# Four graph layers in one kernel: the fourth layer's transposes taken from TensorE to VectorE squares and DMAs, and the second layer's Newton step to GpSimd

## The chip, the cores and the metric

The kernel runs on one core of a Trainium2 chip. The metric is the device time of one execution in microseconds (us); the median of three runs of the kernel before is 2920.45 us (2920.34 to 2920.62). A profile is one execution recorded instruction by instruction on the engines of the core: TensorE (PE for matmuls, PEld for loading its weights), VectorE (DVE), ScalarE (ACT), GpSimd (POOL) and SyncE (SP, which here only starts DMAs).

## The reference, cut to what matters

A graph of N = 4096 nodes with 256 features passes through four layers. Each adds its result to its input and normalises each row:

```python
x = _layernorm(x + _L0_gnn_ref(x, adj, W0, a0))               # four heads, additive scores
x = _layernorm(x + _L1_gnn_ref(x, adj, Wq, bq, Wk, bk, Wv, bv))  # four heads, dot products
x = _layernorm(x + _L2_gnn_ref(x, adj, W2, a2))               # one head, additive scores
x = _layernorm(x + _L3_gnn_ref(x, adj, Wq3, Wk3))             # cosine scores
```

The fourth layer is the one that the change is mostly about:

```python
Qn = _cos_normalize(features @ Wq.T)      # 4096 x 128, rows of length 1
Kn = _cos_normalize(features @ Wk.T)
raw_att = Kn @ Qn.T                       # 4096 x 4096
att = jax.nn.softmax(jnp.where(adj > 0, raw_att, NEG), axis=1)
prop_fea = att @ features
return 0.5 * prop_fea + 0.5 * features
```

The layernorm divides by the root of the variance. The kernel gets the inverse root as exp(-0.5 ln v) on ScalarE and improves it by one Newton step, r (1.5 - 0.5 v r r): the four small instructions of `end_root`.

## The kernel before, in words

The features stay in SBUF for the whole run, in X: 32 tiles of 128 rows (nodes), 256 columns and one column of twos. Every layer walks over 8 blocks b of 512 target nodes, and within a block over the source tiles. One step of the walk is a unit (b, j): get the weights of the source tile j for the targets of block b (ScalarE), mask them by the adjacency (VectorE), multiply them with the values and add into PSUM (TensorE). In layers one, three and four a block has 32 units of 128 sources; in layer two 64 units of 64 sources. The sums run one to three units behind the weights.

**Layer two** (`multi_head_attention`, lines 509 to 782). TensorE makes scores (L622) and sums (L655), ScalarE takes the exponential (L624), VectorE masks (L634). The sums of weights for the softmax are gathered in den: GpSimd adds every even unit (L641), an accumulating DMA started by GpSimd adds every odd one (L647). What is left to do for block b - 1 is strewn into the units of block b by `finish`: the variance is ready at unit 29 (`begin_root`, L151, and ScalarE's L130 and L131), `end_root` (L137 to L140) stands at unit 33 of the block, and the scaling of the four row tiles (L155) at 35, 37, 39 and 41. The order on PE, DVE and ACT is the order of the program there (`manual_schedule`); GpSimd's instructions are placed by the scheduler.

**Layer three** (`additive_one`, lines 382 to 506). ScalarE makes e (L432), VectorE masks it to prob (L434), TensorE adds 4 x (128x128)x(128x257) products per unit into PSUM (L440). There are three buffers of prob. PE's order is that of the program; the other engines' orders are the scheduler's. SP loads the masks (L430). In block b the outputs of block b - 1 are finished at units 0, 4, 8 and 12.

**Layer four** is prepared by the class `Cosine` for a block b in three steps (`prepare`, L810):
- step 0: `transposed_block` turns the 4 x 2 squares of 128x128 of the features by TensorE with the identity (L118) into two PSUM banks, which VectorE and ScalarE copy to xT (L120);
- step 1: TensorE multiplies xT with the weights of q and k (L823), ScalarE takes the squares of the rows' lengths (L828), VectorE copies the rows (L829), makes the inverse root (L831, L137 to L140) and scales (L834);
- step 2: TensorE turns q and k (L840), ScalarE copies them to T (L841), which holds q and k of all nodes, turned.

Six of the blocks are prepared in the last block of layer three: step 0 of block n at unit 4n, step 1 at 4n + 2, step 2 at 4n + 5 (L497), so that a turn of four units of sums holds one of each. Blocks 6 and 7 are prepared within the first block of layer four itself, at units 1, 3, 6 and 12, 14, 17 (L892). The masks of layer four are loaded by GpSimd's queue (L808), the first three behind layer three's units 6, 10 and 14 (`behind`, which makes GpSimd copy a number of the unit first, L91).

**The walk of layer four** (`cosine_attention`): scores T x T (L864, into banks p and g), exponential (L867), mask (L868), sums with X (L875). The outputs are stored by SP (L888), and y, their buffer, is filled by ScalarE (L905).

Of the kernel before, what the change touches and what calls it, by code (L numbers as in the profile page):

```python
# [9 lines left out]
FP = mybir.dt.float32  # L10
# [4 lines left out]
OP = mybir.AluOpType  # L15
# [3 lines left out]
P = 128  # L19
D = 256  # L20
KC = D // P
QB = 4
QW = QB * P
# [5 lines left out]
def kernel(  # L29
# [81 lines left out]

    def transposed_block(sb, bank, b, copies=(nc.vector.tensor_copy, nc.scalar.copy)):

        xT = sb.tile([P, KC, QW], FP, name="xT")
        pts = [bank() for _ in range(KC)]
        for c, pt in enumerate(pts):
            for k in range(QB):
                nc.tensor.transpose(pt[:, k * P:(k + 1) * P], X[:, b * QB + k, c * P:(c + 1) * P], ident)  # L118
        for c, pt in enumerate(pts):
            copies[c](xT[:, c, :], pt)  # L120
        return xT

    def one_row(mv, k, y):
        st = fin.tile([P, 6], FP, name="bn")
# [6 lines left out]
        nc.scalar.activation(r, r, AF.Exp, scale=-0.5)  # L131
        return r

    def end_root(v, r, n):

        s = fin.tile([P, n], FP, name=f"s{n}")
        nc.vector.tensor_tensor(s, r, r, OP.mult)  # L137
        nc.vector.tensor_tensor(s, s, v, OP.mult)
        nc.vector.tensor_scalar(s, s, -0.5, 1.5, OP.mult, OP.add)  # L139
        nc.vector.tensor_tensor(r, r, s, OP.mult)  # L140

    def inverse_root(v, n):

# [26 lines left out]
    def additive_values(xT, b, groups, w_sb, V, src, dst, H, slope):  # L170

        g = 1.0 - slope
        heads = "p k (h d) -> p k h d"
        for k, n, pw in groups:
            for c in range(KC):
                for i in range(n):
                    nc.tensor.matmul(pw[:, i, :D + 2 * H], xT[:, c, (k + i) * P:(k + i + 1) * P], w_sb[:, c, :],  # L177
                                     start=(c == 0), stop=(c == KC - 1))
            t = slice(b * QB + k, b * QB + k + n)
            s, d = pw[:, :, D:D + H], pw[:, :, D + H:D + 2 * H]  # L180
            nc.scalar.activation(src[:, t, :], s, AF.Exp, scale=g)
            nc.scalar.activation(dst[:, t, :], d, AF.Exp, scale=g)
            nc.scalar.activation(V[:, t, D:], d, AF.Exp, scale=slope)
            nc.vector.tensor_tensor(V[:, t, :D].rearrange(heads, h=H), pw[:, :, :D].rearrange(heads, h=H),
                                    V[:, t, D:].unsqueeze(3).to_broadcast([P, n, H, D // H]), OP.mult)
# [196 lines left out]
    def additive_one(w_sb, slope, tail, op, follow):  # L382
# [3 lines left out]
        with ExitStack() as lay:  # L386
# [76 lines left out]
            with tc.manual_schedule(engines={mybir.EngineType.PE}):  # L463
                xTs = {0: turn(0), 1: turn(1)}
                project(0, xTs[0])
                project(1, xTs[1], [0, 1])
                fill_row(0)
                project(1, xTs[1], [2, 3])
                for i in range(len(units) + 1):
                    if i < len(units):  # L470
                        b, j = units[i]
                        weights(b, j)

                        if b == 0 and j // QB + 2 < NB:
                            n = j // QB + 2
                            if j % QB == 0:
                                xTs[n] = turn(n)
                            elif j % QB == 2:
                                project(n, xTs[n])
                                fill_row(n)  # L480
                    if i:
                        b, j = units[i - 1]
                        sums(b, j)
                        if (b, j) == (0, 1):
                            fill_row(1)
                        if b == 0 and j in (0, 3, 5):
                            tail(bank, (0, 3, 5).index(j))
                            if j == 5:
                                follow.start()
                        if b and j % 4 == 0 and j // 4 < QB:  # L490
                            outputs(b - 1, j // 4)
                        if b == NB - 1:
                            if j in (6, 10, 14):
                                follow.load_mask(0, (j - 6) // 4, prob[b, j][:, :1])


                            for step, first in enumerate((0, 2, 5)):  # L497
                                if j >= first and (j - first) % 4 == 0 and (j - first) // 4 < NB - 2:
                                    follow.prepare(even_bank, (j - first) // 4, step)
                        if j == NT - 1:  # L500
                            take_all(b)
# [7 lines left out]
    def multi_head_attention(w_sb, b_sb, tail, rows_of_den, narrow_edges):  # L509
# [12 lines left out]
        with ExitStack() as lay:  # L522
# [7 lines left out]
            with ExitStack() as pro:  # L530
# [14 lines left out]
                def keys(b):  # L545
                    for n, to, scale in (("k", kT, 1.0), ("q", qT, qscale)):
                        for o in range(KC):
                            pk = bank()
                            for c in range(KC):
                                nc.tensor.matmul(pk, w_sb[n][:, c, o * P:(o + 1) * P], xTs[b][:, c, :],  # L550
                                                 start=(c == 0), stop=(c == KC - 1))
                            part = to[:, o, b * QW:(b + 1) * QW]
                            nc.scalar.activation(part, pk, AF.Identity, bias=b_sb[n][:, o:o + 1], scale=scale)
                            nc.vector.tensor_reduce(big[n][:, b, o:o + 1], part, AX.X, OP.max,
                                                    apply_absolute_value=True)

                def values(b):


                    for k in range(0, QB, KC):  # L560
                        pv = pv2.tile([P, KC, D], FP, name="pv")
                        for s in range(KC):
                            for c in range(KC):
                                nc.tensor.matmul(pv[:, s, :], xTs[b][:, c, (k + s) * P:(k + s + 1) * P], w_sb["v"][:, c, :],  # L564
                                                 start=(c == 0), stop=(c == KC - 1))
                        j = 2 * (b * QB + k)
                        for n in range(2):
# [149 lines left out]
            def finish(b, j):  # L717
# [12 lines left out]
                elif j == 18:  # L730
                    half(turned_half(halves(), b, 2), b, 2)
                elif j in (21, 23, 25, 27):
                    k = (j - 21) // 2
                    if k == 0:
                        mvs[b] = fin.tile([P, QB, 2], FP, name="mv")
                    one_row(mvs[b], k, rows[k])
                elif j == 29:
                    roots[b] = begin_root(mvs[b])
                elif j == 33:
                    end_root(*roots[b])  # L740
                elif j in (35, 37, 39, 41):
                    k = (j - 35) // 2
                    scale_row(rows[k], mvs[b], roots[b][1], k)
# [41 lines left out]
    class Cosine:  # L785
# [7 lines left out]
        def start(self):  # L793
# [1 line left out]
            self.pool = self.stack.enter_context(tc.tile_pool(name="co_in", bufs=2, side="right", reuse_waits="tile"))  # L795
            self.masks = self.stack.enter_context(tc.tile_pool(name="co_mask", bufs=4, side="right", reuse_waits="tile"))
            self.mask = {}
            self.T = keep.tile([P, 2, N], FP, name="T")
            self.w_sb = keep.tile([P, KC, 2 * P], FP, name="w3_sb")
            load_w(self.w_sb[:, :, :P], wq3T, nc.sync)  # L800
            load_w(self.w_sb[:, :, P:], wk3T, nc.sync)
# [7 lines left out]

        def prepare(self, bank, b, step):  # L810

            in_, w_sb, T = self.pool, self.w_sb, self.T
            if step == 0:
                self.xT[b] = transposed_block(in_, bank, b)
            elif step == 1:
                xT = self.xT.pop(b)
                norm = in_.tile([P, QB, 2], FP, name="norm")
# [1 line left out]
                for k in range(0, QB, 2):  # L819
                    pr = bank().rearrange("p (t n f) -> p t n f", t=2, f=P)  # L820
                    for t in range(2):
                        for c in range(KC):
                            nc.tensor.matmul(pr[:, t, :, :], xT[:, c, (k + t) * P:(k + t + 1) * P], w_sb[:, c, :],  # L823
                                             start=(c == 0), stop=(c == KC - 1))
                    for t in range(2):
                        for n in range(2):
# [7 lines left out]
                nc.vector.tensor_tensor(flat, flat, r.unsqueeze(2).to_broadcast([P, QB * 2, P]), OP.mult)  # L834
            else:
                rows = self.rows.pop(b)
                for n in range(2):
                    pt = bank()
                    for k in range(QB):
                        nc.tensor.transpose(pt[:, k * P:(k + 1) * P], rows[:, k, n, :], ident)  # L840
                    nc.scalar.copy(T[:, n, b * QW:(b + 1) * QW], pt)  # L841

    def cosine_attention(co, tail):
        MJ = co.MJ
        T, in_ = co.T, co.pool
        with ExitStack() as lay:
            sb = pool(lay, "co_sb", 3)

            pa = pool(lay, "co_pa", 1, space=PSUM)
            pz = pool(lay, "co_pz", 2, space=PSUM)  # L850
# [5 lines left out]
                return ps.tile([P, QW], FP, name="g")  # L856

            def weights(b, j):
                cols = slice(b * QW, (b + 1) * QW)
                m = b, j // MJ  # L860
                if m not in co.mask:
                    co.load_mask(*m)
                p = bank() if b and j % 2 else pz.tile([P, QW], FP, name="p")
                nc.tensor.matmul(p, T[:, 0, j * P:(j + 1) * P], T[:, 1, cols], start=True, stop=True)  # L864

                z = prob[b, j] = sb.tile([P, QW], FP, name="prob")
                nc.scalar.activation(z, p, AF.Exp)  # L867
# [21 lines left out]

            units = [(b, j) for b in range(NB) for j in range(NT)]  # L890
            LAG = 2
            steps = {(0, j + n): (NB - 2 + b, step) for b, j in enumerate((1, 12)) for step, n in enumerate((0, 2, 5))}  # L892
            for i in range(len(units) + LAG):
                if i < len(units):
                    b, j = units[i]
# [5 lines left out]
                if i >= LAG:  # L901
                    b, j = units[i - LAG]
                    if j == NT - 8:
                        y[b] = in_.tile([P, QB, D], FP, name="y")
                        nc.scalar.mul(y[b], X[:, b * QB:(b + 1) * QB, :D], 1.5)  # L905

                    if i < len(units):
# [93 lines left out]
```

## Time and profile before

| what | value |
|---|---|
| median of three runs | 2920.45 us |
| the profiled execution | 2920.01 us |
| its span, first to last instruction | 2918.1 us |
| granted TensorE clock | 0.999 |
| VectorE's masking in layer two, L634, 512 times | 1223 ns each |
| GpSimd's addition in layer two, L641, 248 times | 2495 ns each |
| TensorE per product of layers three and four with 257 columns (two records, from start to start) | 0.434 us |
| DVE, ACT, POOL busy in a turn of layer three's last block (2190 to 2202 us) | 6.3, 7.0, 0 of 12 us |
| POOL busy in a block of layer two (1103 to 1217 us) | 101 of 114 us |
| TensorE waiting for L634 in all | 5.6 us, 8 times |

A line of the profile names an engine, a source line, an operation, "out<-in" by the names of the tiles, a shape and how often it ran. The chain of work goes back from the last instruction, at each step to what released it, so an engine's share of the chain is what it holds of the time. The table of DMAs gives the size in KB and the median time from issue to landing, where it is known. A busy PE is a rough measure, since matmuls overlap and their ends are modelled: distances between starts are taken instead.

### The profile page before, as it was taken

How to read it: one execution, taken by the hardware profiler on the slowest of the kernel's cores; microseconds unless marked ns; L12 is line 12 of the kernel's file. 1: busy time of each engine (PE TensorE's matmuls, PEld its weight loads, DVE VectorE, ACT ScalarE, POOL GpSimd, SP SyncE). 2: the span in 40 equal slices, each digit the busy share in tenths (PEclk: the TensorE clock that was granted, in tenths of full speed). 3: DMA queues.
4: the chain of work that ended last, by engine and by line, in shares of the span. 5: the costliest groups of instructions: out<-in, count | busy, mean ns of one | idle time of the engine just before them, and what ended most of it. 6: DMA issues, size and time to landing. Idle time of an engine off the chain costs nothing.

```text
span 2918.1 us, 50377 instructions
## 1 busy us (share of the span) xinstructions
PE 2901.0 (99%) x20269; PEld 1564.5 (54%) x20269; DVE 1959.0 (67%) x2545; ACT 1668.3 (57%) x2613; POOL 927.0 (32%) x647
## 2 busy tenths in 40 slices
PE   9999999999999999999999999999999999999998
PEld 5333333333643333333333358888888777777776
DVE  8899999997677877877877765555655323333333
ACT  7899999997356666666666654444454222222222
POOL 0010010100068888988889860000000000000000
PEclk9999999999999999999999999999999999999999
DMA  7566666664068888889889874444442333333331
GB/s 204 107 135 140 136 140 142 135 134 84 1 142 191 182 187 189 181 186 191 180 189 188 184 164 138 153 152 150 154 136 60 49 58 58 58 58 58 58 58 29
DMA packets 207148, 374.94 MB, mean 128 GB/s; under 512 B 15057, under 2 KB 90817, under 8 KB 206018
## 3 DMA queue, kind: packets, MB, share of 16 engines
q0 software_dynamic: 102304, 177.77, 38.5%
q1 hardware_dynamic: 104336, 193.69, 20.2%
q8 instruction: 159, 2.61, 0.3%
q14 instruction: 75, 0.61, 0.1%
q10 hardware_dynamic: 274, 0.26, 0.0%
HBM read 317.07 MB, written 21.04 MB: 116 GB/s over the span
## 4 chain that ended last, share of the span: by engine, by line
PE 97%; DVE 2%; ACT 0%; issue 0%; DMA 0%; DVEq 0%; SPq 0%
PE acc L274 23%; PE acc L875 15%; PE p L622 15%; PE acc L655 14%; PE acc L440 8%; PE g L440 8%; PE p L864 4%; PE g L864 3%; PE g L550 2%; PE g L177 1%; PE pv L564 1%; PE g L118 1%; PE acc L823 1%; PE acc L177 1%; DVE prob L634 1%; DVE s L139 1%
## 5 line engine op out<-in xcount | busy, mean ns | idle before, releaser
L634 DVE TENSOR_TENSOR prob<-p,mask 128x1024 f32<-128x1024 f32 x512 | 623.0, 1223 | 197.2 <-ACT p L624 193.4
L624 ACT ACTIVATE p<-p,shift 128x1024 f32<-128x1024 f32 x512 | 556.2, 1088 | 331.9 <-PE p L622 331.0
L274 PE MATMUL acc<-prob,V 128*32 128x512 f32 x6144 | 664.0, 592 | 1.2 <-DVE prob L264 1.2
L641 POOL TENSOR_TENSOR den<-den,prob 128x1024 f32<-128x1024 f32 x248 | 618.8, 2495 | 72.4 <-DVE prob L634 62.9
L261 ACT ACTIVATE prob<-row,dst 128x512 f32<-128x512 f32 x1020 | 633.2, 712 | 0.1
L264 DVE SCALAR_TENSOR_TENSOR prob<-prob,mask 128x2048 f32<-128x2048 f32 x256 | 582.7, 2288 | 24.1 <-ACT prob L261 20.4
L622 PE MATMUL p<-qT,kT 64*64 64x512 f32 x4096 | 532.7, 590 | 5.6 <-DVE prob L634 5.6
L655 PE MATMUL acc<-prob,V 64*64 64x512 f32 x4096 | 531.5, 589 | 0.0
L875 PE MATMUL acc<-X,prob 128*128 128x257 f32 x2048 | 485.2, 380 | 0.0
L875 PEld LDWEIGHTS acc<-X,prob 128*128 128x128 f32 x2048 | 388.5, 190 | 160.7 <-issue 113.4
L868 DVE TENSOR_TENSOR prob<-prob,mask 128x512 f32<-128x512 f32 x256 | 176.5, 691 | 418.8 <-ACT prob L867 417.6
L274 PEld LDWEIGHTS acc<-prob,V 128*32 128x32 f32 x6144 | 197.3, 110 | 453.1 <-issue 434.2
L91 POOL COPY tick<-prob 128x1 f32<-128x1 f32 x35 | 39.8, 1136 | 1017.5 <-DVE prob L264 644.3
L432 ACT ACTIVATE e<-row,dst 128x512 f32<-128x512 f32 x256 | 184.2, 722 | 235.1 <-DVE prob L434 209.0
L655 PEld LDWEIGHTS acc<-prob,V 64*64 64x64 f32 x4096 | 155.9, 133 | 285.3 <-issue 278.1
L622 PEld LDWEIGHTS p<-qT,kT 64*64 64x64 f32 x4096 | 153.7, 133 | 284.4 <-issue 255.7
L434 DVE SCALAR_TENSOR_TENSOR prob<-e,mask 128x512 f32<-128x512 f32 x256 | 178.5, 698 | 185.7 <-PE acc L440 94.5
L808 POOL DMA_DIRECT2D mask<-in_adjT x64 | 47.5, 743 | 633.8 <-DVE prob L868 509.7
L647 POOL DMA_DIRECT2D den<-prob x240 | 225.9, 941 | 28.0 <-DVE prob L634 21.0
L867 ACT ACTIVATE prob<-p 128x512 f32<-128x512 f32 x144 | 85.8, 596 | 260.1 <-PE p L864 246.0
L440 PE MATMUL g<-V,prob 128*128 128x257 f32 x1024 | 225.6, 380 | 0.0
L440 PE MATMUL acc<-V,prob 128*128 128x257 f32 x1024 | 225.1, 380 | 0.0
(154 smaller groups left out, 1972.2 us busy)
## 6 DMA issues: line engine op xcount, KB each, us to landing
mask<-in_adjT SPq DMA_DIRECT2D x256, 512.0 KB
den<-prob POOLq DMA_DIRECT2D x240, 512.0 KB, 5.3
mask<-edges SPq DMA_DIRECT2D x256, 128.0 KB
mask<-in_adjT POOLq DMA_DIRECT2D x64, 512.0 KB, 5.6
edges<-in_adj POOLq DMA_DIRECT2D x32, 512.0 KB, 9.8
den<-prob SPq DMA_DIRECT2D x16, 512.0 KB
row<-far SPq DMA_DIRECT2D x7, 1024.0 KB
X<-in_x SPq DMA_DIRECT2D x7, 512.0 KB
```

The source lines that it names most:

```text
L261: nc.scalar.activation(z[:, h, :], r, AF.Relu, bias=-1.0, scale=dst[:, j, h:h + 1])
L264: nc.vector.scalar_tensor_tensor(z, z, 1.0, mask[m][:, j % MJ, :].unsqueeze(1).to_broadcast([P, H, QW]), OP.add, OP.mult)
L274: nc.tensor.matmul(acc[b][h * G:(h + 1) * G, n, :], part, prob[b, j][:, h, :], start=(j == 0), stop=(j == NT - 1))
L440: nc.tensor.matmul(acc[b][k][:, :D + 1], prob[b, j][:, k * P:(k + 1) * P], V[:, j, :], start=(j == 0), stop=(j == NT - 1))
L622: nc.tensor.matmul(p[c * d:(c + 1) * d, r, :], kT[half, c, j * d:(j + 1) * d], qT[half, c, cols], start=True, stop=True)
L624: nc.scalar.activation(p, p, AF.Exp, bias=shift)
L634: nc.vector.tensor_tensor(z, p, mask[m][:, j % MJ, :].unsqueeze(1).to_broadcast([P, KC, QW]), OP.mult)
L641: nc.gpsimd.tensor_tensor(to, to, flat, OP.add)
L647: nc.gpsimd.dma_start(to, flat, accum_op=OP.add)
L655: nc.tensor.matmul(acc[b][c][r * d:(r + 1) * d, :], V[half, j, r * d:(r + 1) * d], prob[b, j][half, r, :], start=(j == 0), stop=(j == NH - 1))
L864: nc.tensor.matmul(p, T[:, 0, j * P:(j + 1) * P], T[:, 1, cols], start=True, stop=True)
L875: nc.tensor.matmul(acc[b][k], prob[b, j][:, k * P:(k + 1) * P], X[:, j, :], start=(j == 0), stop=(j == NT - 1))
```

## The change

Two independent edits.

*Fourth layer.* The transposes by TensorE go. A new function `turned_apart` turns 128 rows x 512 columns in three parts: VectorE transposes each 32x32 square in place (its own `transpose`), a DMA writes the squares to DRAM, and four DMAs read them back, 32 partitions each, so that every square stands where the whole transpose has it. It is used for the features (step 0) and for the rows of q and k (step 2). The place of the columns differs from before, so xT and T have a new layout, and T becomes eight tiles, one a block. Blocks 0 to 5 start their DMAs on GpSimd, blocks 6 and 7 on SP. There is one buffer of squares on chip, and there are two in DRAM. Step 0 is called six units earlier than before in layer three (units 26 and 30 of the block before the last for the first two), and in layer four the steps stand at units 1, 6, 9 and 12, 17, 20. `transposed_block` keeps TensorE for the other layers; only the shape that it returns has changed.

*Second layer.* `end_root` takes an engine. In `finish` it stands at unit 31, not 33, and runs on GpSimd.

```diff
+    def turned_apart(once, dr, part, to, eng):
+        B = P // QB
+        squares = once.tile([P, QB, KC, P], FP, name="squares")
+        for c in range(KC):
+            nc.vector.transpose(squares[:, :, c, :].rearrange("p q (k n) -> p k q n", n=B),
+                                part(c).rearrange("p k (q f) -> p k q f", f=B))
+        far = dr.tile([QB, B, QB, KC * P], FP, name="squares_far")
+        eng.dma_start(far.rearrange("a f q m -> (a f) (q m)"), squares.rearrange("p q c m -> p (q c m)"))
+        for q in range(QB):
+            eng.dma_start(to[q * B:(q + 1) * B], far[:, :, q, :].rearrange("a f m -> f a m"))
+        return to.rearrange("p a (c m) -> p c a m", c=KC)
...
-    def end_root(v, r, n):
+    def end_root(v, r, n, eng=nc.vector):
         s = fin.tile([P, n], FP, name=f"s{n}")
-        nc.vector.tensor_tensor(s, r, r, OP.mult)
-        nc.vector.tensor_tensor(s, s, v, OP.mult)
-        nc.vector.tensor_scalar(s, s, -0.5, 1.5, OP.mult, OP.add)
-        nc.vector.tensor_tensor(r, r, s, OP.mult)
+        eng.tensor_tensor(s, r, r, OP.mult)
+        eng.tensor_tensor(s, s, v, OP.mult)
+        eng.tensor_scalar(s, s, -0.5, 1.5, OP.mult, OP.add)
+        eng.tensor_tensor(r, r, s, OP.mult)
...
+                        n, rest = divmod(i - (NB - 1) * NT + 5, 4)
+                        if rest == 0 and 0 <= n < NB - 2:
+                            follow.prepare(even_bank, n, 0)
...
-                            for step, first in enumerate((0, 2, 5)):
+                            for step, first in enumerate((2, 5), 1):
...
-                elif j == 33:
-                    end_root(*roots[b])
+                elif j == 31:
+                    end_root(*roots[b], nc.gpsimd)
...
+            eng = nc.gpsimd if b < NB - 2 else nc.sync
             if step == 0:
-                self.xT[b] = transposed_block(in_, bank, b)
+                self.xT[b] = block_apart(in_, self.once, self.dram, b, eng)
...
-                for n in range(2):
-                    pt = bank()
-                    for k in range(QB):
-                        nc.tensor.transpose(pt[:, k * P:(k + 1) * P], rows[:, k, n, :], ident)
-                    nc.scalar.copy(T[:, n, b * QW:(b + 1) * QW], pt)
+                turned_apart(self.once, self.dram, lambda n: rows[:, :, n, :], self.T[b], eng)
...
-                nc.tensor.matmul(p, T[:, 0, j * P:(j + 1) * P], T[:, 1, cols], start=True, stop=True)
+                nc.tensor.matmul(p.rearrange("p (k i) -> p k i", k=QB), T[j // QB][:, 0, j % QB], T[b][:, 1],
+                                 start=True, stop=True)
...
-            steps = {(0, j + n): (NB - 2 + b, step) for b, j in enumerate((1, 12)) for step, n in enumerate((0, 2, 5))}
+            steps = {(0, j + n): (NB - 2 + b, step) for b, j in enumerate((1, 12)) for step, n in enumerate((0, 5, 8))}
```

In the changed kernel the squares are made at L130, written at L133 and read back at L135, the projection of q and k is L852, the masking of layer three L453, the scores of layer four L889, and L137 to L140 have become L156 to L159.

More of the change, by code (lines that the diff above doesn't have):

```diff
@@ L112, in transposed_block @@
     def transposed_block(sb, bank, b, copies=(nc.vector.tensor_copy, nc.scalar.copy)):
-        xT = sb.tile([P, KC, QW], FP, name="xT")
+        xT = sb.tile([P, KC * QW], FP, name="xT").rearrange("p (c i) -> p c i", c=KC)
         pts = [bank() for _ in range(KC)]
@@ L120, in transposed_block, with block_apart @@
             copies[c](xT[:, c, :], pt)
-        return xT
+        return xT.rearrange("p c (k i) -> p c k i", i=P)
+    def turned_apart(once, dr, part, to, eng):
[9 more added lines that the diff above has]
+        return to.rearrange("p a (c m) -> p c a m", c=KC)
+    def block_apart(sb, once, dr, b, eng):
+        xT = sb.tile([P, KC * QW], FP, name="xT").rearrange("p (a m) -> p a m", a=QB)
+        return turned_apart(once, dr, lambda c: X[:, b * QB:(b + 1) * QB, c * P:(c + 1) * P], xT, eng)
     def one_row(mv, k, y):
@@ L176, in additive_values @@
                 for i in range(n):
-                    nc.tensor.matmul(pw[:, i, :D + 2 * H], xT[:, c, (k + i) * P:(k + i + 1) * P], w_sb[:, c, :],
+                    nc.tensor.matmul(pw[:, i, :D + 2 * H], xT[:, c, k + i], w_sb[:, c, :],
                                      start=(c == 0), stop=(c == KC - 1))
@@ L549, in keys @@
                             for c in range(KC):
-                                nc.tensor.matmul(pk, w_sb[n][:, c, o * P:(o + 1) * P], xTs[b][:, c, :],
+                                nc.tensor.matmul(pk, w_sb[n][:, c, o * P:(o + 1) * P],
+                                                 xTs[b][:, c].rearrange("p k i -> p (k i)"),
                                                  start=(c == 0), stop=(c == KC - 1))
@@ L563, in values @@
                             for c in range(KC):
-                                nc.tensor.matmul(pv[:, s, :], xTs[b][:, c, (k + s) * P:(k + s + 1) * P], w_sb["v"][:, c, :],
+                                nc.tensor.matmul(pv[:, s, :], xTs[b][:, c, k + s], w_sb["v"][:, c, :],
                                                  start=(c == 0), stop=(c == KC - 1))
@@ L797, in start @@
             self.mask = {}
-            self.T = keep.tile([P, 2, N], FP, name="T")
+            self.T = [keep.tile([P, QB, 2 * P], FP, name=f"T{b}") for b in range(NB)]
+            self.dram = self.stack.enter_context(tc.tile_pool(name="co_dram", bufs=2, space=bass.MemoryType.DRAM))
+            self.once = self.stack.enter_context(tc.tile_pool(name="co_once", bufs=1, side="right", reuse_waits="tile"))
             self.w_sb = keep.tile([P, KC, 2 * P], FP, name="w3_sb")
@@ L810, in prepare @@
         def prepare(self, bank, b, step):
-            in_, w_sb, T = self.pool, self.w_sb, self.T
+            in_, w_sb = self.pool, self.w_sb
+            eng = nc.gpsimd if b < NB - 2 else nc.sync
             if step == 0:
-                self.xT[b] = transposed_block(in_, bank, b)
+                self.xT[b] = block_apart(in_, self.once, self.dram, b, eng)
             elif step == 1:
@@ L822, in prepare @@
                         for c in range(KC):
-                            nc.tensor.matmul(pr[:, t, :, :], xT[:, c, (k + t) * P:(k + t + 1) * P], w_sb[:, c, :],
+                            nc.tensor.matmul(pr[:, t, :, :], xT[:, c, k + t], w_sb[:, c, :],
                                              start=(c == 0), stop=(c == KC - 1))
@@ L836, in prepare @@
                 rows = self.rows.pop(b)
-                for n in range(2):
-                    pt = bank()
-                    for k in range(QB):
-                        nc.tensor.transpose(pt[:, k * P:(k + 1) * P], rows[:, k, n, :], ident)
-                    nc.scalar.copy(T[:, n, b * QW:(b + 1) * QW], pt)
+                turned_apart(self.once, self.dram, lambda n: rows[:, :, n, :], self.T[b], eng)
     def cosine_attention(co, tail):
         MJ = co.MJ
-        T, in_ = co.T, co.pool
+        T = [t.rearrange("p k (n i) -> p n k i", n=2) for t in co.T]
         with ExitStack() as lay:
             sb = pool(lay, "co_sb", 3)
+            yp = pool(lay, "co_y", 2)
             pa = pool(lay, "co_pa", 1, space=PSUM)
@@ L858, in weights @@
             def weights(b, j):
-                cols = slice(b * QW, (b + 1) * QW)
                 m = b, j // MJ
@@ L903, in cosine_attention @@
                     if j == NT - 8:
-                        y[b] = in_.tile([P, QB, D], FP, name="y")
+                        y[b] = yp.tile([P, QB, D], FP, name="y")
                         nc.scalar.mul(y[b], X[:, b * QB:(b + 1) * QB, :D], 1.5)
```

## The prediction

> **What bounds the kernel.** I read first the page's busy line and its chain of work, to see which engine sets the end:
>
> ```profile
> PE 2901.0 (99%) x20269; PEld 1564.5 (54%) x20269; DVE 1959.0 (67%) x2545; ACT 1668.3 (57%) x2613; POOL 927.0 (32%) x647
> PE 97%; DVE 2%; ACT 0%; issue 0%; DMA 0%; DVEq 0%; SPq 0%
> ```
>
> TensorE is 97% of the chain, so an instruction taken off it is time saved wherever nothing new makes it wait. Then the chain inside the last block of the third layer, where six of the eight blocks of the fourth layer are prepared (columns: start us, us, what):
>
> ```profile
> 2158.98 3.47 PE g L440 x16
> 2162.45 0.87 PE acc L118 x8
> 2163.32 1.74 PE g L440 x8
> 2165.06 0.87 PE acc L840 x8
> 2165.93 1.74 PE g L440 x8
> 2167.67 3.45 PE acc L823 x16
> 2171.12 3.47 PE g L440 x16
> ```
>
> One turn: four units of sums (L440, 1.735 each), eight transposes of features (L118, 0.87), a projection (L823, 3.45), eight transposes of q and k rows (L840, 0.87). The pieces abut: nothing else is waited for. Next, the 2% of DVE on the chain. It stands in layer two, seven times alike, once per block; the chain and the timeline there:
>
> ```profile
> 992.58 2.52 DVE s L139
> 995.21 1.24 DVE prob L634
> ...
> 992.44 2.62 POOL L641 TENSOR_TENSOR den<-den,prob 128x1024 f32<-128x1024 f32 x1
> 992.58 2.51 DVE L139 TENSOR_SCALAR s<-s 128x4 f32<-128x4 f32 x1
> 996.49 1.09 PE L622 MATMUL p<-qT,kT 64*64 64x512 f32 x8 [0.67 <-DVE prob L634]
> ```
>
> L139, the third step of Newton on 128x4 numbers, lasts 2.51 us; in layer three it lasts 0.17. It ends with GpSimd's addition beside it, and 0.67 of its delay reaches TensorE.
>
> **The change, part by part.** Line numbers are those before unless said.
>
> *Transposes removed.* 8 blocks x 16 = 128 on TensorE, 0.87/8 = 0.109 us each: 13.9 us, 10.4 in layer three's last block and 3.5 in the fourth layer's first, both all TensorE on the chain. A turn falls from 12.13 to 10.39. The bound below zero gain is excluded, since no matmul is added; the strided reads of T are still runs of 128 numbers.
>
> *Copies removed.* Per block one on DVE (0.68) and three on ACT (0.59). ACT was busy 7.0 of 12 us per turn, so nothing is gained there.
>
> *Newton step to GpSimd.* Four small operations leave DVE seven times. Gain: the 0.67 us of TensorE, 7 x 0.67 = 4.7. It costs GpSimd four operations; its nearest row is the 128x1 copy in layer three at 0.19 to 0.22, so 1 us with waits, 2 us at worst, per block. GpSimd is busy 101 of 114 us per block, so this has cover. In the built order the four stand behind the addition of the unit before L151, at about 988 us; queued behind them are the accumulating DMAs and additions of den. The scaling that needs the root is DVE's at 997.5: nine us of cover. I take the full 4.7; the other end is 0, if GpSimd's new phase puts another small DVE operation under an addition. The Trainium skill speaks against this move: "GPSIMD Engine Reference", Engine selection, keeps elementwise work on VectorE, GpSimd being about twice as slow. By the rule 4 x 0.17 becomes some 1.4 us; but the row has DVE pay 2.51 for one of them, and the page "SBUF — State Buffer", Who interferes with whom, says why: a tensor_scalar in a two-port mode and a GpSimd instruction exclude each other for the whole instruction. The row decides.
>
> *Squares, added.* For each of 16 turnings: two VectorE transposes 128x512, one DMA of 512 KB to DRAM, four DMAs of 128 KB back, which wait for it. No row shows the VectorE transpose; the nearest is a 128x512 copy at 0.69 (L829), the same number of elements per lane. From 0.6 to 1.4 (two passes); I take 0.69, with starts 0.6 apart as those of the masking are. VectorE was busy 6.3 of 12.1 us per turn; now about 6.3 - 0.7 + 2.5 of 10.4, which fits, but not its waits: there is one buffer of squares, so each pair waits until the DMA of the pair before has landed, and the masking of the next units is queued behind.
>
> *The DMAs.* GpSimd issues for six blocks: each turning costs it one issue, the wait for landing, four issues at 0.54 (L418's row). The nearest row for the write W is out<-y, also 512 KB from SBUF to DRAM, but issued by SP; its landing is when ACT may overwrite y:
>
> ```profile
> 2338.20 0.38 SPq L888 DMA_DIRECT2D out<-y  x1
> 2343.30 1.06 ACT L905 ACTIVATE y<-X 128x1024 f32<-128x1024 f32 x1 [2.82 <-DMA out<-y]
> ...
> mask<-in_adjT POOLq DMA_DIRECT2D x64, 512.0 KB, 5.6
> row<-far POOLq DMA_DIRECT2D x6, 256.0 KB, 6.2
> far<-src POOLq DMA_DIRECT2D x6, 2.0 KB, 10.2
> ```
>
> 5.1 us there, and 5.4 to 6.5 the five other times. The Trainium skill ("DMA: Bandwidth & Descriptors", Anatomy of one DMA) gives 2.0 us plus bytes over 436 GB/s: 3.2 for the write, 2.3 for a 128 KB read. The other end is far<-src, 10.2 us, also to DRAM from GpSimd, but in 4-byte pieces. The new write is in pieces of 4 KB, larger than out<-y's 1 KB: I take W = 5.0. For the reads R, between 2.3 and row<-far's 5.2 (its fastest, twice the bytes): 4.5. The last of four lands 1.6 + R after W.
>
> *Where they must be ready.* Time zero is the first sums of layer three's last block. Without waits the projections n = 0 to 5 start at 5.2 + 10.39 n: 5.2, 15.6, 26.0, 36.4, 46.8, 57.2. Step 0 is called six units earlier than before, and in the built order the features of blocks 0 to 2 are turned blocks earlier, so n = 0, 1 are ready; the reads of n = 2 wait for a buffer until projection 0 ends, 8.7, and land by 16.
> - Rows of block 0 (T0): squares at about 14.3; written by 19.3, read by GpSimd to 21.5.
> - Features 3: VectorE waits for 19.3, done 20.6; write 21.5 to 26.5; in place 32.6. Due 36.4: in time by 4. VectorE's masking for unit 10, behind it, is done at 22.3, due 24.3.
> - T1: squares 30.8; write to 36; GpSimd free at 38.2.
> - Features 4: VectorE reaches them only behind the masking of unit 17, which waits for sums 14 to end (36.4): squares 38.3. Write 38.4 to 43.4; in place 49.5. Due 46.8: **2.7 us late**.
> - T2: VectorE reaches it behind unit 21, so after sums 18 (46.8): squares 48.8, write to 53.8.
> - Features 5: squares wait for 53.8; GpSimd reads T2 until 56; write to 61; in place 67.2. Due 57.2 + 2.7 = 59.9: **7.3 us late**.
> - T3 to T5 are due 30 us later, and blocks 6 and 7 go over SP's queue, in which only layer three's last mask loads stand ahead and the stores of the outputs behind, with some 12 us from squares to projection against W + 1.6 + R = 11: no wait, 1 at worst.
>
> New waits: 10.0 us. Span: 2918.1 - 13.9 - 4.7 + 10.0 = 2909.5. The profiled execution took 2920.01 (1.9 outside the span), the median of the runs 2920.45; so 2911.4, or 2911.8 against the median. I say 2911.5. In such a sum W counts about four times: 0.3 us of W is over a microsecond.
>
> **Rivals.** 0.2% is 5.8 us, about what a measurement of this kernel can tell from no change: below 2914.6 is faster, above 2926.3 slower.
> - *Forecast*: gain 18.6, waits 7 to 13: 2909 to 2915. For it: the rows of 5.1 to 5.6.
> - *Nearly hidden*: W 3.2, R 2.3, as the skill's fit has it. Features 4 are in time; features 5 are in place at 61.6, 4.3 late: 2920.4 - 18.6 + 4.3 = 2906; with no wait at all 2902. Against it: no 512 KB DMA in this trace lands under 5.
> - *Gain eaten*: VectorE transposes at 1.4 us (+3), reads issued at 0.9 as the den DMAs are (+3), or Newton without gain (+4.7): waits of 13 to 24, 2915 to 2926.
> - *Slower*: one mechanism, the DRAM write landing as far<-src does. With W = 10 and R = 5 features 3 come 4 late, the masking of units 10 and 14 a further 5, features 4 and 5 some 14 each: 35 us, so 2937. It decides from W of about 7 on, where the waits reach 18.6. For it: DMA share is 0.5 to 0.6 in this stretch, with SP's mask loads among it. Against: those masks from GpSimd still land in 5.6 there, and far<-src is 512 pieces of 4 bytes.
> - *It does not do what it says* is excluded for the transposes: the built program has 128 fewer on TensorE.
>
> **Chances.** Forecast 0.44, nearly hidden 0.23, eaten 0.20, slower 0.13. Faster 0.67, same 0.20, slower 0.13. Range 2903 to 2922: it leaves out the slower case and the outer edges of the hidden and eaten ones.
>
> **What would show it.** Right: waits of TensorE's projection (L852 in the changed kernel) for DMAs into xT, two large ones, growing from block 4 to 5; squares waiting on VectorE; no 2.5 us operation of VectorE in layer two, and its blocks 0.67 shorter. Wrong: projections 4 and 5 without wait (W overrated), or already 3 (underrated); a VectorE transpose far from 0.69; a 2.5 us L170 or L174; TensorE waiting for masking (L453) behind the squares by more than 1 us in all.

## The result and the profile after

The changed kernel takes 2911.62 us (median of 8 runs, 2910.26 to 2913.24) beside 2920.28 us for the kernel before (8 runs): a ratio of 0.9972, 95% interval 0.9962 to 0.9981. The forecast was 2911.5 us. The profiled execution took 2912.43 us, with a span of 2910.7 us against 2918.1 us.

The page's busy line, its chain, and from its table of DMAs the row of the squares (KB each, median us from issue to landing):

```profile
PE 2889.4 (99%) x20141; PEld 1553.4 (53%) x20141; DVE 1954.2 (67%) x2541; ACT 1655.3 (57%) x2589; POOL 965.2 (33%) x735
PE 98%; DMA 1%; DVE 1%; ACT 0%; issue 0%; POOL 0%; DVEq 0%; POOLq 0%
...
squares_far<-squares POOLq DMA_DIRECT2D x12, 512.0 KB, 4.0
```

TensorE has 128 instructions fewer. DVE's share of the chain has gone from 2% to 1%, and DMA, which had none, has 1%. Where that DMA stands is seen from the first start of each layer's matmuls in the two traces:

| stretch | before, us | after, us | change | sum of the prediction |
|---|---|---|---|---|
| up to layer two's scores | 815.7 | 816.3 | +0.6 | 0 |
| layer two | 917.2 | 910.8 | -6.4 | -4.7 |
| layer three | 503.1 | 505.1 | +2.0 | -10.4 + 10.0 |
| layer four | 682.1 | 678.5 | -3.6 | -3.5 |

In layer two the Newton step is on GpSimd, and no VectorE operation of 128x4 is held up. The timeline, at the place of the 2.51 us L139 of before:

```profile
985.94 0.16 DVE L170 TENSOR_SCALAR v<-mv 128x4 f32<-128x4 f32 x1
...
989.07 0.19 POOL L158 TENSOR_SCALAR s<-s 128x4 f32<-128x4 f32 x1
```

What TensorE waited for (us in all, times, longest):

```profile
PE acc L852 <- DMA xT<-squares_far: 8.7, 2, 7.9
...
PE p L645 <- DVE prob L657: 0.8, 1, 0.8
```

The second line is what is left of the 5.6 us, 8 times, that TensorE waited for L634 before. The first is new. In the chain of layer three's last block it looks like this (start us, us, what):

```profile
2149.11 3.45 PE acc L852 x16
2152.57 6.94 PE g L459 x32
2159.51 3.45 PE acc L852 x16
...
2173.64 1.31 DVE squares L130 x2
...
2175.23 7.20 DMA squares_far<-squares
...
2185.20 8.59 DMA squares_far<-squares
...
2195.96 3.61 DMA xT<-squares_far
```

One turn without waits is now 2159.51 - 2149.11 = 10.4 us, as computed. Then the chain leaves TensorE: squares of the rows of block 1 (T1), their write, their reads on GpSimd, the write of the features of block 4 behind them, the reads. The projections of blocks 3 and 4 in PE's timeline (the brackets give the idle time before):

```profile
2181.28 3.69 PE L852 MATMUL acc<-w_sb,xT 128*128 128x256 f32 x16 [0.79 <-DMA xT<-squares_far]
2199.81 6.55 PE L852 MATMUL acc<-w_sb,xT 128*128 128x256 f32 x16 [7.90 <-DMA xT<-squares_far]
```

The projection of block 5 follows at 2213.13 without a wait. And that of block 4 itself took 6.55 us where the others take 3.6. The table by windows shows why (the three last columns are the granted clock, the share of the DMA engines and GB/s):

```profile
2176.00:2186.00 10.00, 9.21 (x43) 7.80 (x42) 5.98 (x12) 5.04 (x21) 4.48 (x8) 1.00 1.10 279
2186.00:2196.00 10.00, 5.91 (x28) 4.82 (x26) 6.47 (x13) 3.51 (x8) 1.67 (x4) 0.97 1.03 292
2196.00:2206.00 10.00, 6.19 (x16) 5.01 (x17) 2.00 (x3) 1.14 (x8) 3.81 (x7) 0.52 0.65 207
```

After 7.9 us of idleness TensorE was granted 0.52 of its clock in this window (0.55 during the projection alone). The slow projection costs 6.55 - 3.62 = 2.9 us. So layer three's +2.0 is -10.4 (transposes) + 8.7 (waits) + 2.9 (slow projection) + 0.8 that is not placed.

The same windows offer a theory, **A**: the DMA share is above 1 where the squares are late, with two mask loads of layer four issued by GpSimd at 2176.8 amid them and layer three's masks from SP. The rival, **B**: the chain over one buffer of squares, VectorE's order and GpSimd's queue is too long whatever else moves. A third, **C**: the Newton step alone makes the gain.

### The profile page after: what moved, and what is told of

The parts are those of the page before. It is cut to its first block, busy times and chain, and to the rows that moved or that the text cites. A ratio compares the mean times of both kernels' runs of the same rounds, so it can differ in the third digit from the quotient of the medians.

```text
span 2910.7 us, 50256 instructions
## 1 busy us (share of the span) xinstructions
PE 2889.4 (99%) x20141; PEld 1553.4 (53%) x20141; DVE 1954.2 (67%) x2541; ACT 1655.3 (57%) x2589; POOL 965.2 (33%) x735
## 4 chain that ended last, share of the span: by engine, by line
PE 98%; DMA 1%; DVE 1%; ACT 0%; issue 0%; POOL 0%; DVEq 0%; POOLq 0%
PE acc L293 23%; PE acc L901 15%; PE acc L678 15%; PE p L645 15%; PE acc L459 8%; PE g L459 7%; PE p L889 4%; PE g L889 3%; PE g L572 2%; PE g L196 1%; PE pv L587 1%; PE acc L196 1%; PE g L118 1%; PE acc L852 1%; DMA squares_far<-squares 1%; PE g L305 0%
## 5 line engine op out<-in xcount | busy, mean ns | idle before, releaser
L647 ACT ACTIVATE p<-p,shift 128x1024 f32<-128x1024 f32 x512 | 556.2, 1088 | 325.2 <-PE p L645 324.4
L664 POOL TENSOR_TENSOR den<-den,prob 128x1024 f32<-128x1024 f32 x248 | 626.9, 2528 | 72.6 <-DVE prob L657 64.7
L453 DVE SCALAR_TENSOR_TENSOR prob<-e,mask 128x512 f32<-128x512 f32 x256 | 177.6, 695 | 173.4 <-PE acc L459 93.9
```

The source lines that it names most:

```text
L647: nc.scalar.activation(p, p, AF.Exp, bias=shift)
L664: nc.gpsimd.tensor_tensor(to, to, flat, OP.add)
```

## The experiments

Each time stands beside the kernel before, measured together with it (2919.85 us for e1 to e4, 2920.14 for e5 to e8, 2919.75 for e9 to e11, 2919.81 for e12). Single runs of one kernel spread by 0.7 to 5.6 us. A landing is counted from the issue of a DMA to its end; GpSimd goes on about 0.5 us after it.

**e1, the Newton step alone**, in the kernel before:

```diff
-                elif j == 33:
-                    end_root(*roots[b])
+                elif j == 31:
+                    end_root(*roots[b], nc.gpsimd)
```

> The kernel before with only the Newton step moved to GpSimd and to unit 31; layer four as before. By the two traces layer two became 0.89 us shorter per block, seven times, so 6.2 us: 2914.1. By the prediction's sum 4.7: 2915.6. By the rival that all of the gain comes from here and the squares bring nothing: 8.7, so 2911.6. A gain of GpSimd's slowness being felt elsewhere would show as less than 3.

Measured 2912.94: 6.9 faster, ratio 0.9977 (0.9968 to 0.9986), which is 4.1 to 9.3 us. C's 8.7 is not excluded by this run, and 4.7 is inside too.

**e2, the squares alone**: the changed kernel with `end_root` at unit 33 on VectorE.

> The changed kernel with the Newton step back on VectorE at unit 33. If the two edits add up: 2911.6 + 6.2 = 2917.8, with the 7.9 us wait of the projection of block 4 and its slow clock as in the changed kernel. By the rival that the squares bring nothing: 2920.3. By the prediction's sum: 2916.3.

Measured 2917.26: 2.6 faster, ratio 0.9991 (0.9985 to 0.9998), with the wait of 7.9 and the projection of 6.45 us. The edits add up within their spread; C falls, narrowly (the interval is 0.6 to 4.4 us): the squares do bring something, but 2.6 of their 13.9.

**e3, layer four's first masks out of the way**:

```diff
+                        if b == NB - 2 and j in (6, 10, 14, 18):
+                            follow.load_mask(0, (j - 6) // 4, prob[b, j][:, :1])
-                            if j in (6, 10, 14):
-                                follow.load_mask(0, (j - 6) // 4, prob[b, j][:, :1])
```

> The changed kernel with the four first mask loads of layer four behind units 6, 10, 14 and 18 of the block before, so that they are out of the way of the squares. Theory A (the DMA engines are full, and the masks fill them): the write of T1 and of features 4 falls from 7.2 and 8.6 to about 4, their reads from 8 to about 4; the wait of 7.9 and the slow clock of 3.1 go: 2901 to 2903, or a few us more if features 5, due earlier again, are late. Rival B (the chain over one buffer of squares, VectorE and GpSimd is too long by itself): landings within 1 us of what they were, a wait above 5 stays: 2909 to 2912.

Measured 2909.83 (0.9967, 0.9954 to 0.9979). A, in the form that these masks were to blame, falls: the wait for features 4 is 8.7, and the projection after it takes 6.70. GpSimd's timeline (write issued, then the idle time until it may read):

```profile
2172.48 0.56 POOL L133 DMA_DIRECT2D squares_far<-squares  x1
2180.38 2.19 POOL L135 DMA_DIRECT2D T<-squares_far  x4 [7.33 <-DMA squares_far<-squares]
2182.56 0.56 POOL L133 DMA_DIRECT2D squares_far<-squares  x1
```

The write of T1 still landed only after 7.6 us (its first read starts 2180.38 - 2172.48 = 7.9 us after the issue), at a DMA share of 0.79 in place of 1.03. What was left beside it were the squares' own reads and layer three's masks.

**e4, features a turn earlier**, with three buffers for them:

```diff
-                        n, rest = divmod(i - (NB - 1) * NT + 5, 4)
+                        n, rest = divmod(i - (NB - 1) * NT + 9, 4)
...
+            self.xTs = self.stack.enter_context(tc.tile_pool(name="co_xT", bufs=3, side="right", reuse_waits="tile"))
```

> The changed kernel with three buffers for the turned features, each block's features begun four units (7 us) earlier. Theory A and rival B both let the wait of 7.9 and the slow clock of 3.1 go, or fall below 2, so 2900 to 2903, but differ in the landings: by A the writes beside the masks still take 7 to 9 us, by B they are as before the change of place because only their order counts. If instead the masking of layer three (L453) or the rows become late in its place, TensorE shows new waits and the time stays above 2907.

Measured 2901.05 (0.9938, 0.9925 to 0.9950), 18.8 faster. The landings are as long as before (T1 7.4, a write of features 8.9, share up to 1.10); TensorE waits 0.6 in all for features. Both theories foresaw the time. It shows that nothing else was late behind these waits.

**e5, without layer three's mask loads** (from unit 8 of its last block on):

```diff
-                if j % MJ == 0:
+                if b == NB - 1 and j >= 8:
+                    mask[m] = mask[b, 3]
+                elif j % MJ == 0:
```

> The changed kernel without layer three's mask loads from unit 8 of its last block on (the mask of units 6 and 7 is used again, so the outputs differ). With layer four's masks out of the way (e3) the write of T1 and of features 4 still took 7.9 and 8.3 us. Theory A2 (the squares and the mask loads on SP share the DMA engines, and this makes a landing 7 to 8 us instead of 3 to 4): the writes fall to 3 to 5, the wait of 7.9 falls below 2 and the slow clock goes: 2900 to 2903. Rival B (a chain of one buffer and one GpSimd queue in order is too long whatever else moves): a wait above 5 stays, 2908 to 2912.

Measured 2905.57 (0.9953, 0.9938 to 0.9967). In between: the write of T1 fell to 2.9, that of features 4, with two of layer four's masks issued ahead of it, to 5.7; TensorE waits 3.0 for features 4 and 1.6 for features 5:

```profile
2195.40 5.29 PE L854 MATMUL acc<-w_sb,xT 128*128 128x256 f32 x16 [2.98 <-DMA xT<-squares_far]
2209.18 3.69 PE L854 MATMUL acc<-w_sb,xT 128*128 128x256 f32 x16 [1.56 <-DMA xT<-squares_far]
```

Other transfers do lengthen the landings, but a wait remains.

**e6, two buffers of squares**:

```diff
-            self.once = self.stack.enter_context(tc.tile_pool(name="co_once", bufs=1, side="right", reuse_waits="tile"))
+            self.once = self.stack.enter_context(tc.tile_pool(name="co_once", bufs=2, side="right", reuse_waits="tile"))
```

> The changed kernel with two buffers of squares on chip, so that VectorE need not wait for the write before, and the write of the features can stand in GpSimd's queue ahead of the reads of the rows. Rival B: the chain through T1 is broken, features 4 are in place some 8 us earlier, the wait and the slow clock go: 2900 to 2903. Theory A2: the same bytes move at the same time; the landings stay 7 to 9 us or grow and only 1 to 3 us of the wait go: 2907 to 2911.

Measured 2902.51 (0.9943, 0.9927 to 0.9960), as B has it: one wait of 1.4 is left, with all mask loads in place and a DMA share of 1.03 to 1.09 in every window from 2160 to 2210. VectorE's timeline shows what the second buffer changed:

```profile
2168.35 1.30 DVE L130 STREAM_TRANSPOSE squares<-rows 128x512 f32<-128x512 f32 x2
2169.57 1.26 DVE L130 STREAM_TRANSPOSE squares<-X 128x512 f32<-128x512 f32 x2
2179.64 1.30 DVE L130 STREAM_TRANSPOSE squares<-rows 128x512 f32<-128x512 f32 x2
2180.86 1.26 DVE L130 STREAM_TRANSPOSE squares<-X 128x512 f32<-128x512 f32 x2
```

Two pairs of squares per turn, abutting. In the built order of VectorE they stand behind the masking of units 7, 7, 11, 11, 16, 16; with one buffer behind 7, 9, 13, 17, 21, 21: one pair per turn between units 9 and 21, where each turn needs two.

**e7, TensorE kept busy in the wait**:

```diff
+                if b == 4:
+                    pf = bank()
+                    for n in range(8):
+                        nc.tensor.matmul(pf, w_sb[:, 0, :P], w_sb.rearrange("p c f -> p (c f)"), start=True, stop=True)
```

> The changed kernel with eight matmuls of 128x512, 0.87 us each, that serve nothing, ahead of the projection of block 4, in the time that TensorE waits there. If the slow clock (0.52, the projection 6.55 instead of 3.5 us) comes from the idle 7.9 us, the projection takes 3.5 to 3.7 us at a clock near 1: 2911.6 - 3.1 = 2908.5. If it comes from something else that happens then (transfers, VectorE), it stays above 6 us and the time is 2911 to 2913.

Measured 2915.73 (0.9985, 0.9978 to 0.9992), slower than the changed kernel, which neither side expected. PE's timeline:

```profile
2200.19 3.69 PE L856 MATMUL acc<-w_sb,xT 128*128 128x256 f32 x16 [0.99 <-DMA xT<-squares_far]
...
2214.89 5.38 PE L856 MATMUL acc<-w_sb,xT 128*128 128x256 f32 x16 [4.06 <-DMA xT<-squares_far]
```

The idleness was the cause of the slow clock: with it filled the projection takes 3.69, at a granted clock of 1.00. But features 5 are now late by 4.06, and their projection is slow in turn. They are due 2.3 us sooner than in the changed kernel, where the loss at block 4 had covered them, and are in place 2.3 later: their write landed 0.9 later, and the last read took 5.2 us for 3.8. Of the four reads, the two before 2209.05 took 2.9 and 3.0, the two after it 5.0 and 5.2; SP issues a mask load of layer three at 2209.10, which came at 2211.58 in the changed kernel. That this load lengthens the reads is not tested.

**e8, only the features by squares**: the rows turned by TensorE as before the change.

> The changed kernel with the rows of q and k turned by TensorE again and only the features by squares. That puts 8 x 0.87 = 7.0 us back on TensorE and takes half of the transfers and half of the hops out of the chain. By A2 and by B alike features 4 come in time: the Newton step's 6.9 stays (by its own run), 7.0 of the 13.9 stays, so 2919.9 - 6.9 - 7.0 = 2906.0. If the features alone are too slow through DRAM, a wait stays: above 2909.

Measured 2907.51 (0.9957, 0.9942 to 0.9972): 12.6 faster, no wait for features.

**e9, no other mask loads in the stretch**: the diffs of e3 and e5 together.

> Both: layer four's first four masks loaded in the block before, and no mask loads of layer three from unit 8 of its last block on (one mask used again, so the outputs differ). One buffer of squares and one queue as in the changed kernel. If other transfers are what makes the chain too long: writes of 3 to 4 us throughout, no wait of TensorE for features above 1 us, no slow clock, 2899 to 2902. If the chain is too long with landings of 3.5 also: counted from e5 (squares of features 4 at 2182.8, written by 2188, read by 2190, in place at 2193, due 2192.4) 0.7 us late, and if more than 3 is left, the chain alone is to blame.

Measured 2908.87 (0.9963, 0.9949 to 0.9976). The writes land in 2.9 to 3.9, at a DMA share of 0.30 to 0.49, and features 4 come in time (0.2). But features 5 are 6.1 late, where my sum had none above 1. VectorE's timeline:

```profile
2169.70 1.30 DVE L130 STREAM_TRANSPOSE squares<-rows 128x512 f32<-128x512 f32 x2
2180.09 1.30 DVE L130 STREAM_TRANSPOSE squares<-X 128x512 f32<-128x512 f32 x2
2190.48 1.30 DVE L130 STREAM_TRANSPOSE squares<-rows 128x512 f32<-128x512 f32 x2
2195.10 1.31 DVE L130 STREAM_TRANSPOSE squares<-X 128x512 f32<-128x512 f32 x2 [3.32 <-DMA squares_far<-squares]
```

and PE's:

```profile
2206.72 5.61 PE L853 MATMUL acc<-w_sb,xT 128*128 128x256 f32 x16 [6.09 <-DMA xT<-squares_far]
```

T1, features 4, T2 are exactly one turn (10.39) apart, and none of them waits for a landing: their place in VectorE's order holds them back. Features 5 then wait 3.32 for the buffer, until T2's write has landed, and their own write stands in GpSimd's queue behind T2's reads:

```profile
2195.29 2.19 POOL L135 DMA_DIRECT2D T<-squares_far  x4 [2.65 <-DMA squares_far<-squares]
2197.47 0.56 POOL L133 DMA_DIRECT2D squares_far<-squares  x1
```

So the chain through one buffer is enough for one large wait, even with the quickest landings; how much of it is VectorE's order, how much the buffer's own wait and how much GpSimd's queue stays open. Features 5 are in place 58.7 us after the projection of block 0 starts; in e5 it is 58.5, but there the wait of block 4 had already taken a part.

**e10, only the rows by squares**: `transposed_block` for the features, at the units of before.

> The changed kernel with the features turned by TensorE again and only the rows of q and k by squares: the other half of e8. If either half alone is free and only both in one chain are late: 2920.1 - 6.9 - 7.0 = 2906.2, no wait for T or xT, writes of 4 to 6 us beside the mask loads. If the rows' trips are what is slow by themselves: landings above 7 as in the changed kernel, still hidden, the same time. A time above 2909 would say that the rows cost VectorE or GpSimd something that TensorE feels.

Measured 2905.84 (0.9953, 0.9937 to 0.9968): 13.9 faster, no wait, though one write took 7.9 us: hidden.

**e11, e4 and e6 together**, with three mask buffers in layer three in place of four, to make room.

> Two buffers of squares and three of turned features, each block's features begun four units earlier; layer three has three mask buffers in place of four to make room. With all 128 transposes gone, the Newton step's 6.9 kept and no wait: 2920.0 - 13.9 - 6.9 = 2899.2. If layer three's masks come late with three buffers, waits of TensorE for L453 of some us show and the time is above 2901 (e4 had 2901.1, e6 2902.5).

Measured 2901.90 (0.9939, 0.9927 to 0.9952). No wait for features, but one of 2.9 for a masking in layer three (L453), as foreseen for three mask buffers. The trace has the mask behind it:

```profile
1807.94 1.29 DVE L453 SCALAR_TENSOR_TENSOR prob<-e,mask 128x512 f32<-128x512 f32 x2 [6.52 <-DMA mask<-in_adjT]
1808.68 3.74 PE L459 MATMUL acc<-V,prob 128*128 128x257 f32 x16 [2.86 <-DVE prob L453]
```

With four mask buffers (the changed kernel, e4) VectorE's L453 waits for no mask.

**e12, e3 and e6 together**.

> Two buffers of squares (e6) and layer four's first four masks loaded in the block before (e3). If other transfers still decide with two buffers: the wait of 1.4 us that e6 left for features 5 goes too, 2920.0 - 13.9 - 6.9 = 2899.2, up to 2901. If the chain of one buffer was all of it, the masks change nothing more: e6's 2902.5 within 1.5 us, with a wait of about 1 us left.

Measured 2900.18 (0.9930, 0.9917 to 0.9944), 19.6 faster, the best of all and faster than the changed kernel by 11. No wait of TensorE in the stretch is left:

```profile
2170.00:2180.00 10.00, 10.00 (x48) 8.77 (x47) 7.70 (x16) 5.25 (x22) 5.14 (x10) 1.00 0.96 303
2180.00:2190.00 10.00, 10.00 (x48) 8.80 (x47) 7.64 (x16) 5.28 (x23) 4.06 (x9) 1.00 0.93 282
```

Six of the eight writes in the stretch still took 5.7 to 9.2 us: with two buffers even slow landings are covered. The masks' transfers were then worth about the 1.4 us of wait that e6 still had; the difference of 2.3 between the two times is within their spread.

**The cases together.** Waits of TensorE for features, with the squares' buffers across and the other transfers down:

| | one buffer | two buffers |
|---|---|---|
| all mask loads | 0.8 (block 3) and 7.9 (block 4) | 1.4 |
| layer four's masks early | 8.7 (block 4) | 0 |
| layer three's mask loads left out | 3.0 (block 4) and 1.6 (block 5) | not tried |
| neither in the stretch | 6.1 (block 5) | not tried |

Neither theory alone: the chain of B sets whether there is a large wait; the load on the DMA engines sets which block it strikes, and moves the sum between 4.5 and 8.7 us. The buffer's own wait and the order that comes of it were not separated by e6, which changes both. Whether GpSimd's queue alone could be the cause, with the same DMAs started by SP, was not tried.

## Why the prediction was right in its number and wrong in its details

- *128 transposes, 13.9.* Right. A turn is 10.4 as computed, layer four's stretch lost 3.6 for 3.5 foreseen. Beside e1's 6.9, the features' half alone gave 5.7 (e8), the rows' half 7.0 (e10), both with two buffers and layer four's masks early 12.7 (e12), with two buffers alone 10.7 (e6), and both with one buffer, as changed, 1.8.
- *Newton, 4.7.* The mechanism was right, the term was too small: layer two's block is 112.80 us for 113.69, 0.89 and not 0.67 shorter, in all 6.4. The waits that the trace names fell by 4.8, 4.7 being foreseen; where the other 1.6 come from is open. The rule against GpSimd that the prediction weighs did not bite: 0.19 to 0.22 us an operation beside 0.16 to 0.17, under cover.
- *VectorE's transpose, 0.69.* It is 0.702 (median of 32). The order of VectorE was right also: features 4 expected at 38.3 after the first sums, so 2182.0; they began at 2182.45, though of this they waited the last 1.15 for T1's landing, which the sum had done by then.
- *W = 5.0 for every write.* This is the step that failed. No one value fits GpSimd's writes: 2.9 to 8.6 in one kernel, 7.2 for T1 and 8.6 for features 4, where the share of the DMA engines passes 1, and 4.0 or less from T2 on. Both ends had been named; that W would change from turn to turn, highest where it mattered, had not. R was 4.5; it is 2.9 to 8.2 in the stretch. Two statements around W were wrong in themselves: a 512 KB DMA does land under 5 in the trace before (the quickest of L647 took 4.5), and W counts in the sum twice, not four times, in T2's write and in that of features 5: the 4.3 of "nearly hidden" for 10.0 come of two W and one R.
- *Features 4 late by 2.7, features 5 by 7.3.* It is 0.8, 7.9 and 0 for blocks 3, 4 and 5. For features 4: the write began 3.0 later than in the sum (T1's own landing), took 3.6 longer, GpSimd took 0.5 to go on, the reads were 0.9 shorter: 6.3 later in place, against a due time 1.4 later. Features 5 were due 9.5 us later than counted (2213.13 for 2203.65), mostly because of block 4. A lateness of theirs was real behind it: in e7, which takes the slow clock away, they are 4.1 late, in e9 6.1.
- *New waits 10.0.* The waits are 8.7, and 2.9 of slow clock come on top, which the sum had no term for: 11.6. Newton's 1.7 more nearly cancels this. That the number fits to 0.1 us is luck.
- *The rivals.* "Nearly hidden" failed, and with quick writes of 2.9 to 3.9 (e9) it would have failed too: features 5 are 6.1 late, where it had 4.3. Of "gain eaten" no mechanism appeared. "Slower" needed W of about 7 in every write; two had it.
- *Layer three's masking behind squares.* No wait of TensorE for L453 stands among those of the changed kernel; VectorE waited 13.6 us (6 times) for the buffer of squares, and only the later squares felt it.

## What to carry to other kernels

When work moves from the bound engine into a chain of queues, count how many trips per turn the order of each queue lets through and compare with how many are needed: here each half alone cost nothing, and both together, through one buffer, gave back 11 of 13 us. A second buffer was worth more here (e6) than quicker transfers (e5, e9), and the built order changed with it. A wait on TensorE hides the lateness of everything due behind it, so removing the first wait alone can gain nothing or, as e7 shows, lose.

## What the hardware showed that was not expected

- After 3.0 us of idleness (as the trace has it, with modelled ends of matmuls) the projection took 5.29 us (e5), after 4.06 5.38 (e7), after 6.1 5.61 (e9), after 7.9 6.55, after 8.7 6.70 (e3), in place of 3.6, at a granted clock of 0.68, 0.67, 0.64, 0.55 and 0.53; after 1.4 to 1.6 us it took 3.69. A long wait of TensorE is thus dearer by 1.7 to 3.1 us than its length. The Trainium skill ("TensorE: Matmul & The Clock Gate", Part 1) has a gate that halves the clock after an idle window of about 3.4 us that runs free of the kernel; the 0.53 and 0.55 agree, and 3.0 us were enough here.
- The same 512 KB write to DRAM lands in 2.9 to 3.9 us with no mask loads beside it (e9), and in up to 8.9 with them (e4), at a DMA share of 1.0 to 1.1. The 3.2 of the fit in the Trainium skill ("DMA: Bandwidth & Descriptors", Anatomy of one DMA) is that of the unloaded case.
